# Rotary query copies in an attention kernel: spread over four heads, and in the first block over two queues

## Chip, cores and metric

The kernel runs on one core of a Trainium2 chip. The metric is the device time of one execution in microseconds; lower is better. Of several executions the median counts. A profiled execution also leaves a trace of every engine: TensorE (PE, matrix products; PEld are its weight loads), VectorE (DVE), ScalarE (ACT), GpSimd (POOL) and SyncE (SP), whose only work here is to issue DMA transfers.

## The reference

One layer of latent attention with 16 heads over 2048 positions of width 512, a layer norm after the residual, a linear layer with its residual and a second layer norm. What matters for the change is the attention: a query and a key have 128 parts without position and 64 parts with rotary position, and the key's rotary part is shared by all heads.

```python
cq = rms_norm(hidden_states @ w_qa.T, q_a_ln_w)
q = (cq @ w_qb.T).reshape(b, s, H, DQ).transpose(0, 2, 1, 3)
q_nope, q_pe = (q[..., :DN], q[..., DN:])
q_pe = q_pe * cos + rotate_half(q_pe) * sin
...
q_full = jnp.concatenate([q_nope, q_pe], axis=-1)
k_full = jnp.concatenate([k_nope, jnp.broadcast_to(k_pe, (b, H, s, DR))], axis=-1)
scores = jnp.einsum('bhqd,bhkd->bhqk', q_full, k_full) * scale
scores = jnp.where(causal, -jnp.inf, scores)
attn = jax.nn.softmax(scores.astype(jnp.float32), axis=-1).astype(q_full.dtype)
out = jnp.einsum('bhqk,bhkd->bhqd', attn, v)
```

## The kernel before

**Blocks, pairs, head steps.** The 2048 queries are four blocks of 512 (b = 0 to 3). A block goes through eight pairs of heads (p), a pair through four query tiles of 128 rows (qt), each with two heads (j). One head of one query tile is called a head step here; a pair has eight. In block 0 a pair's two heads are taken together, so there a step covers both. Because of the causal mask a step of block b covers up to 512(b+1) keys, so steps grow longer.

**Precision.** Numbers are carried as a high and a low part. A split makes the high part on ScalarE (line 64, a copy to a narrower format) and the low part on VectorE (line 65, the remainder). A product takes high by high, high by low and low by high.

**A head step.** TensorE computes scores (line 438): three products with the plain parts (`Kn,qn`) and two with the rotary parts (`Kp,pe`), where the rotary query stack `pe` of one head holds the high part on partitions 0 to 63 and the low part on 64 to 127. VectorE takes the negative maximum (line 510), ScalarE the exponential (line 532, tile `pr`). The probabilities are split into half-precision high (ScalarE, line 563) and low parts (GpSimd, line 564; lines 598 and 599 in block 0), transposed in squares by VectorE (line 546) back into `pr`, and copied by four DMA transfers (line 553) from `pr` into a ring buffer; in block 3 a step has two such tiles, so eight transfers. TensorE multiplies them with the values (line 619), ScalarE or VectorE copies the result out (lines 625, 628, tile `ot`), and a DMA transfer writes it to `ot_d` in memory.

**The rotary query part.** `project_pe(b, g)` makes it for four heads, that is two pairs: 18 matmuls (line 372, weights `wpe`), products with cosine and sine on VectorE (line 377, tile `prod`), a difference and a sum (lines 383, 384), a split into `ph` and the low part, which overwrites half of `prod`, and eight copies by DMA of 128 KB each into the stack tile `pe`: for every head j of the four its high part, then its low part. `project_nope(b, p)` does the plain part (line 410, weights `wq`). Both are generators, advanced in pieces between head steps, one pair ahead of their use (`project_pe` for the block's next two pairs, or in the block's last pair for the next block).

**Queues.** `state["queue"]` is GpSimd's queue through block 0, and SyncE's afterwards. Weight loads (`wq`, `wpe`, 768 KB each) go by it, and so do the output copies `ot_d`, by `put_off`. In block 0 the ring copies and the eight rotary copies (line 393) are issued by SyncE at the place where they stand. From block 1 on, `put_off(to, src, n)` puts a copy on a list, and `put_in` (line 326), called after the ring copies of each head step, issues by SyncE what has waited n calls and counts the others down; the start of each pair issues whatever is left. The rotary copies have n = 1, so all eight leave together, behind the ring copies of the second step after they were made.

**Numbers of copies.** Five groups are made while the queue is GpSimd's (four for block 0, one for block 1's first pairs), 40 copies; eleven groups follow, 88 copies.

**Order of the work.** In block 0 a scheduler lays out the order of all engines from a model of times. In blocks 1 to 3 the order of TensorE and SyncE, and from early in block 3 that of VectorE and ScalarE, is that of the program text. Every engine works through its instructions in order and waits at the first whose inputs or buffers aren't ready; this holds for the instructions that issue transfers too.

Of the kernel before, what the change touches and what calls it, by code (L numbers as in the profile page):

```python
# [49 lines left out]
def mla_block(ctx: ExitStack, tc: tile.TileContext, a, out):  # L50
    nc = tc.nc
# [9 lines left out]
    def split(ps, h, l, scale=None):  # L61

        if scale is None:
            nc.scalar.activation(h, ps, AF.Copy)  # L64
            nc.vector.tensor_tensor(l, ps, h.bitcast(F32), ALU.subtract)  # L65
        else:
            nc.scalar.activation(h, ps, AF.Copy, scale=scale)  # L67
            nc.vector.scalar_tensor_tensor(l, ps, scale, h.bitcast(F32), ALU.mult, ALU.subtract)  # L68
# [250 lines left out]
    def put_off(dst, src, n=0):  # L319

        if state["queue"] is nc.gpsimd:
            nc.gpsimd.dma_start(dst, src)
        else:
            later.append([n, dst, src])
# [29 lines left out]
    def load_wpe(b, g):  # L354
        if b == NB:
            return
        w = state["wpe", b, g] = prj.tile([P, 2, LT, 256], F32R, tag="wpe", name=f"wpe{b}_{g}")
        move(state["queue"], w, wpe_d[g])

    def project_pe(b, g, direct=None):  # L360

        if direct is None and ("wpe", b, g) not in state:
            load_wpe(b, g)
        w = state.pop(("wpe", b, g)) if direct is None else direct
        cq, cs = state["cq"], state["cs"]
        prod = prj.tile([P, 2, 2, QB], F32, tag="prod", name=f"prod{b}_{g}")
        for x in range(2):
            ps = psum["m"].tile([P, QB], F32, tag="m", name=f"ps_pe{b}_{g}_{x}")
            n = 0
            for lt in range(LT):  # L370
                for i, k in ((0, 0), (0, 1), (1, 0)):
                    nc.tensor.matmul(  # L372
                        ps, w[:, i, lt, x * P : (x + 1) * P], cq[:, k, lt, :], start=n == 0, stop=n == 8
                    )
                    n += 1
            for k in range(2):
                nc.vector.tensor_tensor(prod[:, k, x, :], ps, cs[:, k ^ x, :], ALU.mult)
            if x == 0:
                yield
            elif b or g == 3:  # L380
                load_wpe(*((b, g + 1) if g < 3 else (b + 1, 0)))
        rp, tp = prod[:, 0], prod[:, 1]
        nc.vector.tensor_tensor(rp[:, 0, :], rp[:, 0, :], rp[:, 1, :], ALU.subtract)
        nc.vector.tensor_tensor(rp[:, 1, :], tp[:, 0, :], tp[:, 1, :], ALU.add)
        ph, pl = prj.tile([P, 2, QB], F32R, tag="ph", name=f"ph{b}_{g}"), tp.bitcast(F32R)
        split(rp, ph, pl)
        pe = blk.tile([P, 4, QB], F32R, tag="pe", name=f"pe{b}_{g}")

        for j in range(4):
            for i, part in enumerate((ph, pl)):  # L390
                to, src = pe[64 * i : 64 * i + 64, j, :].bitcast(F32), part[32 * j : 32 * j + 32].bitcast(F32)
                if state["queue"] is nc.gpsimd:
                    nc.sync.dma_start(to, src)
                else:
                    put_off(to, src, 1)
        state["pe", b, g] = pe
        yield

# [24 lines left out]
    def project(b, p):  # L423
        if p % 2 == 0:
            yield from project_pe(b, p // 2)
        yield from project_nope(b, p)
# [249 lines left out]
    for _ in project_pe(0, 0, wpe0):  # L676
        pass
# [20 lines left out]
    def units(pool, ring, b):  # L698
        lag = min(ring.shape[1] // (2048 * (b + 1)) - 1, 3) if b else 2

        for p in range(NPAIR):
# [9 lines left out]
            if b and p % 2 == 0 and p + 2 < NPAIR:  # L711
                fillers.append(project_pe(b, p // 2 + 1))
# [431 lines left out]
```

## Time and profile before

| | |
|---|---|
| median of three executions | 1636.91 us (1634.71 to 1638.35) |
| profiled execution | 1638.56 us |
| its span in the trace | 1636.8 us |
| TensorE busy | 1575.2 us (96%) |
| VectorE, ScalarE, GpSimd busy | 1130.0, 918.3, 846.0 us (69%, 56%, 52%) |
| TensorE's waits for rotary copies (line 438) | 5.5 us, in one piece |
| TensorE's waits for ring copies (line 619) | 5.3 us, in one piece |
| issue of one rotary copy by SyncE in block 0, high or low | median 0.600 us |
| issue of one 128 KB output copy by GpSimd in block 0 | median 0.562 us |
| rotary copies in 245 to 262 us, issue to landing | high 4.3, low 7.9 us (medians of four) |

A row of the page for a group of instructions gives the line, the engine, the operation, output and inputs, shape, count, then busy time in us, the mean duration of one in ns, and the idle time of the engine before these instructions with what ended most of it. In a timeline a row gives start and duration in us, and in brackets the idle time before it and its releaser. PEclk is the share of full clock that TensorE was granted. The slices of the span (40 equal ones, some 41 us each, busy tenths) show where TensorE falls below nine tenths:

```profile
PE   9799998899999999999999999999999998999998
PEclk9899999999999999999999999999999999999999
DMA  6988676676776878787787767867777777962030
```

Block 0 lasts to about 250 us, block 3 begins at about 880 us, and its last result is written out at 1402 us; what is left of the output projection, the norms and the linear layer end the span.

### The profile page before, as it was taken

How to read it: one execution, taken by the hardware profiler on the slowest of the kernel's cores; microseconds unless marked ns; L12 is line 12 of the kernel's file. 1: busy time of each engine (PE TensorE's matmuls, PEld its weight loads, DVE VectorE, ACT ScalarE, POOL GpSimd, SP SyncE). 2: the span in 40 equal slices, each digit the busy share in tenths (PEclk: the TensorE clock that was granted, in tenths of full speed). 3: DMA queues.
4: the chain of work that ended last, by engine and by line, in shares of the span. 5: the costliest groups of instructions: out<-in, count | busy, mean ns of one | idle time of the engine just before them, and what ended most of it. 6: DMA issues, size and time to landing. Idle time of an engine off the chain costs nothing. (4 is left out here: it accounts for less than half of the span.)

```text
span 1636.8 us, 27536 instructions
## 1 busy us (share of the span) xinstructions
PE 1575.2 (96%) x9292; PEld 1294.5 (79%) x9292; DVE 1130.0 (69%) x1874; ACT 918.3 (56%) x1529; POOL 846.0 (52%) x701
## 2 busy tenths in 40 slices
PE   9799998899999999999999999999999998999998
PEld 7688876788888888888887778888887776678876
DVE  5668665577677777777777678778677676575464
ACT  5557564666665757666665665666666654321120
POOL 2345553454554766667765566666666665011011
PEclk9899999999999999999999999999999999999999
DMA  6988676676776878787787767867777777962030
GB/s 213 265 238 267 194 203 164 175 185 172 191 206 171 217 179 202 162 206 181 199 195 180 177 153 174 184 160 160 177 156 192 211 178 210 320 197 77 32 117 33
DMA packets 259436, 297.60 MB, mean 182 GB/s; under 512 B 35264, under 2 KB 227136, under 8 KB 258272
## 3 DMA queue, kind: packets, MB, share of 16 engines
q1 hardware_dynamic: 241008, 251.63, 55.4%
q0 software_dynamic: 11376, 34.52, 12.0%
q10 hardware_dynamic: 6912, 9.70, 2.0%
q8 instruction: 74, 1.21, 0.3%
q14 instruction: 66, 0.54, 0.1%
HBM read 99.94 MB, written 36.44 MB: 83 GB/s over the span
## 5 line engine op out<-in xcount | busy, mean ns | idle before, releaser
L564 POOL TENSOR_TENSOR hlpr<-pr,hlpr 128x1024 f16<-128x1024 f32 (+3 forms) x320 | 613.2, 1935 | 327.2 <-ACT hlpr L563 297.9
L438 PE MATMUL s<-Kn,qn 128*128 128x512 f32 (+4 forms) x1920 | 510.3, 373 | 22.3 <-ACT pr L532 13.9
L532 ACT ACTIVATE pr<-s,bias,rq 128x1024 f32<-128x1024 f32 (+3 forms) x320 | 325.4, 1021 | 343.2 <-issue 178.3
L510 DVE TENSOR_REDUCE neg<-s 128x1 f32<-128x1024 f32 (+3 forms) x320 | 310.0, 985 | 133.2 <-PE s L441 75.0
L438 PEld LDWEIGHTS s<-Kn,qn 128*128 128x128 f32 x1920 | 334.3, 189 | 72.7 <-ACT pr L532 19.9
L619 PE MATMUL o<-ring,V 128*128 128x256 f16 x3024 | 373.1, 273 | 7.4 <-DMA ring<-pr 5.3
L546 DVE STREAM_TRANSPOSE pr<-hlpr 128x1024 f32<-128x1024 f32 (+7 forms) x256 | 311.5, 1223 | 97.9 <-POOL hlpr L564 72.2
L438 PE MATMUL s<-Kp,pe 128*128 128x512 f32 (+4 forms) x1280 | 362.9, 364 | 5.5 <-DMA pe<-prod 5.5
L619 PEld LDWEIGHTS <-V 128*128 128x128 f16 x3264 | 301.1, 96 | 82.7 <-issue 32.0
L563 ACT ACTIVATE hlpr<-pr 128x1024 f16<-128x1024 f32 (+3 forms) x320 | 338.2, 1113 | 4.9 <-DVE pr L546 1.0
L438 PEld LDWEIGHTS s<-Kp,pe 128*128 128x128 f32 x1280 | 233.6, 189 | 36.4 <-DMA pe<-prod 5.7
L410 PE MATMUL ps_qn<-cq,wq 128*128 128x512 f32 x576 | 150.0, 405 | 2.1 <-DMA wq<-wq_d 1.9
L989 POOL TENSOR_TENSOR lnr<-lnt,nhalf 128x1 f32<-128x1 f32 x32 | 21.3, 671 | 213.3 <-DVE lnt L988 213.2
L410 PEld LDWEIGHTS ps_qn<-cq,wq 128*128 128x128 f32 x576 | 105.5, 192 | 23.1 <-DVE xl L65 1.1
L68 DVE SCALAR_TENSOR_TENSOR qn<-ps_qn,kvln,qn 128x512 fp32r<-128x512 f32 x64 | 47.5, 744 | 45.5 <-ACT qn L67 45.2
L599 POOL TENSOR_TENSOR hl<-pr,hl 128x128 f16<-128x128 f32 (+3 forms) x64 | 56.8, 908 | 37.7 <-ACT hl L598 37.3
L372 PE MATMUL ps_pe<-cq,wpe 128*128 128x512 f32 x288 | 75.3, 407 | 0.2 <-DMA cq<-cq_d 0.2
L64 ACT ACTIVATE oh<-o 128x1024 fp32r<-128x1024 f32 x28 | 29.7, 1061 | 79.6 <-PE acc L888 49.1
L888 PE MATMUL acc<-wvo,oh 128*128 128x512 f32 x224 | 71.5, 401 | 1.0 <-ACT pr L532 0.6
L64 ACT ACTIVATE xt<-tp 128x512 fp32r<-128x512 f32 x16 | 9.6, 598 | 94.8 <-PE tp L1008 94.8
L532 ACT ACTIVATION_READ_ACCUMULATOR pr<-s,bias,rq 128x1 f32 x320 | 61.8, 193 | 0.0
L372 PEld LDWEIGHTS ps_pe<-cq,wpe 128*128 128x128 f32 x288 | 53.4, 193 | 10.6 <-issue 0.3
(458 smaller groups left out, 1777.4 us busy)
## 6 DMA issues: line engine op xcount, KB each, us to landing
ring<-pr SPq DMA_DIRECT2D x384, 128.0 KB, 2.9
wq<-wq_d SPq DMA_DIRECT2D x22, 768.0 KB, 6.7
ring<-pr SPq DMA_DIRECT2D x128, 112.0 KB, 3.4
o<-ot_d SPq DMA_DIRECT2D x28, 512.0 KB, 5.5
ot_d<-ot SPq DMA_DIRECT2D x97, 128.0 KB, 2.7
ring<-pr SPq DMA_DIRECT2D x128, 96.0 KB, 2.4
ring<-pr SPq DMA_DIRECT2D x64, 192.0 KB, 4.1
ring<-pr SPq DMA_DIRECT2D x64, 176.0 KB, 5.3
```

Source lines behind the costliest of these rows:

```text
L68: nc.vector.scalar_tensor_tensor(l, ps, scale, h.bitcast(F32), ALU.mult, ALU.subtract)
L372: nc.tensor.matmul(ps, w[:, i, lt, x * P : (x + 1) * P], cq[:, k, lt, :], start=n == 0, stop=n == 8)
L410: nc.tensor.matmul(ps, w[:, i, lt, j * P : (j + 1) * P], cq[:, k, lt, :], start=n == 0, stop=n == 8)
L438: nc.tensor.matmul(ps[:, :w], lhs, K[:, i, c0 : c0 + w], start=n == 0, stop=n == 4 and not by_product)
L510: nc.vector.tensor_reduce(neg[:, ti : ti + 1], v, axis=AX.XY, op=ALU.max, negate=True)
L532: nc.scalar.activation(pr[:, x : x + n * w].rearrange("p (a c) -> p a c", a=n), v, AF.Exp, bias=bias, scale=r, accum_out=sums_of(b, p, qt, ...
L546: nc.vector.transpose(sq.rearrange("p (k c r) -> p k c r", k=4, r=32), words.rearrange("p (c k r) -> p k c r", k=4, r=32))
L563: nc.scalar.activation(hl[:, 0, c], pr[:, c], AF.Copy)
L564: nc.gpsimd.tensor_tensor(hl[:, 1, c], pr[:, c], hl[:, 0, c], ALU.subtract)
L599: nc.gpsimd.tensor_tensor(hl[:, j, 1, :], pr[:, j, :], hl[:, j, 0, :], ALU.subtract)
L619: nc.tensor.matmul(ps[:, :256], vt[:, i, k % 4, :], v[:, :, l, k, :], start=n == 0, stop=n == 3 * kts - 1)
L888: nc.tensor.matmul(acc, l[:, t, c], state["wvo"][p][:, i, j, :], start=p == 0 and j == 0 and n == 0, stop=p == NPAIR - 1 and j == 1 and n ...
```

## The change

In the branch for block 0 (and block 1's first group) the high copy of each head stays with SyncE and the low copy is issued by GpSimd: 20 of the 40 copies change queue. In the branch for blocks 1 to 3 the number of calls that a copy waits is 1 + j in place of 1, so the two copies of head 0 leave behind the step where all eight left, those of heads 1, 2 and 3 behind the next three steps, two at a time. Nothing else is edited; the order of block 0 is laid out anew by the scheduler.

```diff
             for i, part in enumerate((ph, pl)):
                 to, src = pe[64 * i : 64 * i + 64, j, :].bitcast(F32), part[32 * j : 32 * j + 32].bitcast(F32)
                 if state["queue"] is nc.gpsimd:
-                    nc.sync.dma_start(to, src)
+                    (nc.sync, nc.gpsimd)[i].dma_start(to, src)
                 else:
-                    put_off(to, src, 1)
+                    put_off(to, src, 1 + j)
```

In the order of instructions that results, the four low copies of the first group stand on GpSimd right behind the load of the second `wpe` tile, and those of block 1's first group behind a load of `wq` and half of a split of probabilities (line 599).

## The prediction

> **What bounds the kernel now.** I read the page's busy times first, then the costliest groups, then TensorE's waits, and last the timelines of SyncE's queue and of TensorE around the places where those waits stand.
>
> ```profile
> PE 1575.2 (96%) x9292; PEld 1294.5 (79%) x9292; DVE 1130.0 (69%) x1874; ACT 918.3 (56%) x1529; POOL 846.0 (52%) x701
> L438 PE MATMUL s<-Kp,pe 128*128 128x512 f32 (+4 forms) x1280 | 362.9, 364 | 5.5 <-DMA pe<-prod 5.5
> L619 PE MATMUL o<-ring,V 128*128 128x256 f16 x3024 | 373.1, 273 | 7.4 <-DMA ring<-pr 5.3
> ```
>
> TensorE is busy for 1575.2 of 1636.8 us, so nothing that leaves its work alone can win more than 61.6 us. The other two rows name the only long waits that the copies of rotary parts can be behind: one of 5.5 us for a low copy (`pe<-prod`), one of 5.3 us for the ring copies of probabilities, which share SyncE's queue with them. Over long stretches nothing can be won:
>
> ```profile
> 320.00:600.00 280.00, 279.11 (x1719) 230.18 (x1717) 201.41 (x314) 186.85 (x290) 158.80 (x95) 1.00 0.73 188
> 600.00:880.00 280.00, 280.00 (x1724) 230.85 (x1723) 214.21 (x377) 182.52 (x309) 191.02 (x148) 1.00 0.79 193
> 960.00:1240.00 280.00, 280.00 (x1707) 230.24 (x1705) 209.41 (x317) 178.38 (x234) 182.83 (x111) 1.00 0.74 169
> ```
>
> These are the windows by stretch (bounds, length, busy time of PE, PEld, DVE, ACT, POOL, granted clock, DMA share, GB/s). TensorE idles 0.9 us in 840, at full clock, although nine of the eleven bursts of copies of blocks 1 to 3 are issued there. Three places are left: the first score of block 1 (near 252 us), the first burst of block 1 (280 us) and the first of block 3 (913 us), besides block 0 itself.
>
> **Part 1: blocks 1 to 3, two copies behind each head step.** The number of copies stays 88 and each costs SyncE what it did; the starts below are 0.645 us apart, so a pair of them takes 1.29 us. Three pairs (3.87 us) leave the burst and go behind the next three head steps. What stood behind the burst goes earlier: the ring copies of the first step by 3.87 us, of the second by 2.58, of the third by 1.29, of the fourth by nothing. SyncE's timeline of the first burst, and TensorE's beside it:
>
> ```profile
> 280.52 0.61 SPq L330 DMA_DIRECT2D pe<-ph  x1
> 281.17 0.60 SPq L330 DMA_DIRECT2D pe<-prod  x1
> ...
> 285.68 0.58 SPq L330 DMA_DIRECT2D ot_d<-ot  x1
> 286.51 0.56 SPq L59 DMA_DIRECT2D wq<-wq_d  x1
> 287.17 12.72 SPq L553 DMA_DIRECT2D ring<-pr  x16
> ```
>
> ```profile
> 287.28 0.69 PE L438 MATMUL s<-Kn,qn 128*128 128x320 f32 x3
> ...
> 294.33 2.08 PE L619 MATMUL o<-ring,V 128*128 128x256 f16 x9 [5.27 <-DMA ring<-pr]
> 296.06 1.15 PE L438 MATMUL s<-Kn,qn 128*128 128x320 f32 x3
> 297.01 0.73 PE L438 MATMUL s<-Kp,pe 128*128 128x320 f32 x2
> ...
> 298.39 1.16 PE L619 MATMUL o<-ring,V 128*128 128x256 f16 x9
> ```
>
> The probabilities wait for SyncE: their copies start only when eight copies, an output copy and a weight load are through, and TensorE stands 5.27 us. After the wait the rows are slow: 2.08 against 1.16 us, 1.15 against 0.69, 0.73 against 0.46 in an undisturbed row of the same shape, 1.65 us in all; the granted clock is 0.83 over 290 to 300. So the place costs 6.9 us. If every later tile had slack, all of it would go: 3.87 us of the wait at once and with a shorter idle its slow rows too. If none had, TensorE would meet the third step's copies, which come only 1.29 us earlier. The second step's gain, 2.58, lies between and is the next thing TensorE meets (the o matmuls at 298.39 stood without a wait, but close behind). I take -2.6, ends -1.3 and -6.9.
>
> At the start of block 3 the same burst delays ScalarE, whose probabilities want a buffer that the ring copies still read:
>
> ```profile
> 926.11 1.10 ACT L532 ACTIVATE pr<-s,bias,rq 128x896 f32<-128x896 f32 x1 [3.14 <-DMA ring<-pr]
> ...
> 934.43 1.21 ACT L532 ACTIVATE pr<-s,bias,rq 128x1024 f32<-128x1024 f32 x1 [2.38 <-DMA ring<-pr]
> ```
>
> ```profile
> 932.11 0.96 PE L438 MATMUL s<-Kn,qn 128*128 128x512 f32 x3 [0.66 <-ACT pr L532]
> ...
> 948.14 0.72 PE L438 MATMUL s<-Kn,qn 128*128 128x320 f32 x3 [2.31 <-ACT pr L532]
> ...
> 949.98 3.95 PE L619 MATMUL o<-ring,V 128*128 128x256 f16 x21
> ```
>
> Both ScalarE waits are shorter than the 3.87 and about equal to the 2.58 by which those copies move. TensorE loses 0.66 and 2.31 us to late probabilities and 1.45 us to the slow row (3.95 against 2.50 us of the same 21 matmuls at 934.61): 4.4 us. The 2.31 comes 12 us after the last ring wait and may be due to the order around it, not to the copies. I take half of the 4.4, rounded down to -2.0, ends 0 and -4.4.
>
> What is moved behind other work must not be late itself: heads 2 and 3 of a group score a whole pair (eight steps) later than heads 0 and 1, and the last two copies go three steps after the first. Across a block boundary they go one step, about 7 us, before the next group's products overwrite their sources, against a median landing of 2.7 us. I cost this at nothing; its cover is that step, and without it the products at line 377 would wait some 3 us, once at each of two boundaries.
>
> **Part 2: block 0, low copies by GpSimd.** Twenty copies leave SyncE (20 x 0.60 = 12.0 us, by the median row at line 393) and come onto GpSimd. GpSimd's nearest issue is the output copy of the same 128 KB, 0.54 to 0.64, median 0.562 us: 20 x 0.562 = 11.2 us, in 250 us in which it is about half busy, so mostly beside other work. GpSimd is in order: its key additions, its splits of probabilities (line 599) and its output copies stand behind the wait for the low part, which VectorE makes (line 65). The scheduler lays block 0 out anew for all engines. TensorE idles some 15 us there from 60 to 240 us, in pieces under 3 us; I cost the shuffle at 0, ends -3 and +3 (a fifth of that idle).
>
> At the first group the four low copies now stand right behind a weight load of 768 KB in GpSimd's queue, issued at 49.8 and landed 8.8 us later, 58.6. TensorE's first use of the stack is at 58.17, so up to +1; against it ScalarE loses a wait of 1.8 us for such a copy (line 259), which ended in a TensorE wait of 2.75 at 63.05. I take 0, ends -1.8 and +1.
>
> At the boundary the group for block 1 meets the weight load `wq`:
>
> ```profile
> 249.15 0.85 POOL L59 DMA_DIRECT2D wq<-wq_d  x1
> 257.77 0.90 PE L438 MATMUL s<-Kp,pe 128*128 128x320 f32 x2 [5.48 <-DMA pe<-prod]
> wq<-wq_d POOLq DMA_DIRECT2D x1, 768.0 KB, 9.9
> pe<-ph SPq DMA_DIRECT2D x4, 128.0 KB, 4.3
> pe<-prod SPq DMA_DIRECT2D x4, 128.0 KB, 7.9
> ```
>
> The low part is ready at 249.9 (line 65 on VectorE, 248.74 plus 1.18). Issued by SyncE, head 0's copy is used at 257.77; the high ones took 4.3 us, the low ones 7.9 beside the load. The instruction order of the changed kernel puts these four behind that load in the load's own queue. If a queue is served from the front, head 0's copy lands just after the load, 249.15 + 9.9 = 259.05, plus at most 2 us for the copies: +1.3 to +3.2. If the load is quicker, because half the copies that shared the engines with it now stand behind it, or if copies overtake it, the landing is at best that of the high ones, 249.9 + 4.3 = 254.2: -3.5. The load's own row is the nearest, shortened a little: +0.5.
>
> One rule speaks against this part. The Trainium skill, "SBUF — State Buffer", section "A bandwidth-pool intuition that's wrong (but worth ruling out)", says that a transfer issued by GpSimd can be held until VectorE frees a shared port, with about 620 ns alone becoming some 3100. In this trace GpSimd's 31 output copies issue in 0.642 us at most while VectorE is more than half busy, so I see no such hold in the issue. By the page's figure my estimate is 2.5 us more for each copy; with one on the path at each of two places the sum below would be +0.9 in place of -4.1.
>
> **Sum.** 0.5 (boundary) + 0 (first group) + 0 (shuffle) - 2.6 (block 1) - 2.0 (block 3) = -4.1 us. The profiled execution took 1638.56 us (span 1636.8, so 1.8 around it), 1.65 above the median of 1636.91. Against its own time the forecast is 1634.5; carried to the median, **1632.8**. The terms' ends do not all fall together; the forecast's own range is -9 to 0, 1628 to 1637.
>
> **Rivals.** (a) *The stall moves on.* SyncE issues as many copies as before, so the backlog is only put off: block 1 wins its lower end, 1.3, block 3 nothing, and the boundary loses 1.3. For it: 16 ring copies stood in one unbroken row of 12.72 us. Against it: TensorE runs 840 us behind the same bursts without waiting. 0.0, so 1636.9.
>
> (b) *GpSimd's queue is late: slower.* The low copies land behind the 768 KB loads at the first group and at the boundary. The slowest landing from SyncE's put-off copies was 12.4 us; with that, after an issue at 50.5, the first use waits until 62.9 (+4.7), and after one at 251.5, held by the load and a split before it, until 263.9 (+6.1). 10.8 - 4.6 = +6.2: 1643.1. It decides once the two are late by 4.6 + 3.3 = 7.9 us together. For it: the order of that queue. Against it: the load itself took 8.8 and 9.9 us.
>
> (c) *All three places go.* The boundary ends at its best (-3.5, and half of the slow rows behind it, -1.5), blocks 1 and 3 at theirs (-6.9, -4.4): -16.3, 1620.6. For it: SyncE is freed of 12 us in block 0. Against: the copies' order behind the load.
>
> (d) *Nothing on the path changes*, as in the nine bursts that cost nothing; that is (a) in time.
>
> **How the numbers follow.** A difference of 0.2% (3.3 us) is about what a measurement of this kernel can tell from none. Forecast 0.40, (a) with (d) 0.23, (b) 0.25, (c) 0.12. Faster: 0.7 of the forecast and all of (c), with a little of (a), 0.44; slower: (b) and a little of (a) and the forecast's edge, 0.28; the rest, 0.28, is within 0.2%. The range runs from near (c), 1623, to just past (b), 1644; the forecast's own is above.
>
> **What would show it.** Right: the o matmuls near 294 wait less than 2.7 us for ring copies, ScalarE's waits of 3.14 and 2.38 near 926 and 934 shrink, and the first score of block 1 waits 4 to 8 us for a low copy by GpSimd. Wrong: waits for such copies inside block 0 (line 438), a new wait of products at line 377 at a block's start, a longer slow-clock stretch after the boundary, or GpSimd issues well over 0.6 us.

## The result, and the profile after

The changed kernel took 1650.91 us (median of five, 1644.09 to 1652.11) against 1637.54 us for the kernel before in the same comparison: a ratio of 1.007, 95% interval 1.0043 to 1.0097. It is slower by some 13 us where 4 us less were forecast, and lies above the forecast range. A second measurement gave the same ratio, 1.0069 (1.0043 to 1.0095).

The busy times and TensorE's longest waits in the changed kernel (line of the waiting instruction, what it waited for, us in total, times, longest):

```profile
PE 1584.0 (96%) x9292; PEld 1301.9 (79%) x9292; DVE 1136.9 (69%) x1874; ACT 918.5 (56%) x1529; POOL 855.3 (52%) x721
```

```profile
PE s L438 <- DMA pe<-prod: 7.4, 3, 5.9
...
PE ps_pe L372 <- DVE prod L377: 3.5, 1, 3.5
PE ps_qn L410 <- DMA wq<-wq_d: 3.3, 2, 3.1
PE o L619 <- DVE pad L471: 2.8, 1, 2.8
PE o L619 <- DVE prod L377: 2.8, 1, 2.8
```

TensorE has the same 9292 matmuls and is busy 8.8 us longer, at a mean granted clock of 0.985 against 0.990; the clock is lowest behind new waits (0.66 over 165 to 175 us, where the kernel before has 1.00, and 0.83 over 530 to 540). The ring wait of 5.3 us is gone from the top. New are waits behind the products of line 377 and a longest wait of 3.1 us for a weight load (0.9 before). The wait for the first low copy of block 1 is about what it was, 5.9 us.

Where the time goes is read best from how much later TensorE reaches its nth matmul than in the kernel before. The table is worked out from the traces (us; column heads are the times of that matmul before; in block 0 the scheduler changes the order, so there it says how much work was done, not which):

```
                    155    249    268    320    500    560    870    920    970   1360
changed            +2.2   +9.8  +10.6  +10.4  +10.4  +15.5  +16.9  +19.2  +14.3  +14.7
changed, again     +3.2  +10.7  +11.9   +8.0   +7.7  +11.3  +11.3  +13.5   +8.4   +7.6
GpSimd alone       +5.3  +12.9  +12.0  +13.3  +12.7  +13.0  +13.0  +13.3   +8.9   +5.0
spreading alone    +1.1   +3.0   +3.1   -1.2   -0.9   +4.5   +4.5   +5.5   +0.2   -0.9
spread in block    +1.6   +3.9   +3.3   -0.1   -0.2   -0.2   -0.2   -1.6   -6.9   -7.4
GpSimd, in block   +3.9  +11.0   +9.8   +9.0   +9.2   +9.2   +9.2   +7.3   +2.9   +4.8
loads by SyncE     +0.9   +3.1   +1.5   +2.9   +3.2   +3.3   +3.3   +1.3   -1.8   -3.2
one group          +3.6   +4.7   +6.0   +5.6   +5.4   +6.1   +6.1   +5.1   +0.3   +1.6
low first          +2.7   +2.6   +1.7   +3.8   +3.5   +3.3   +3.2   +1.3   -2.2   -4.3
load behind        -0.1   +1.2   -6.1   -4.4   -4.4   -4.4   -4.4   -6.0   -6.4   -5.4
```

Rows below the first belong to the experiments. Read the first: 10 us are lost before block 1, nothing in the first burst, 5 us at the start of block 2, 1.4 us soon after (in this profile alone), 2 us at the start of block 3; 5 us come back right after. Block 0 itself scatters: the rows that keep the order and queues of before (spreading alone, spread in block, low first) stand at +2.6 to +3.9 at 249 us, so the profile of before was at its lower end there, and the price of GpSimd's copies is nearer 8 than 10 us. A single profile is good to some 5 us there: two kernels of the experiments below with the same instructions in block 0 (low copies by ScalarE, without and with spreading) stand at +5.1 and +10.2 at 249 us, and at -4.6 and +0.5 at 268.

### The profile page after: what moved, and what is told of

It is laid out like the page before. It is cut to its first block, busy times and chain, and to the rows that moved or that the text cites. A ratio compares the mean times of both kernels' runs of the same rounds, so it can differ in the third digit from the quotient of the medians.

```text
span 1650.3 us, 27547 instructions
## 1 busy us (share of the span) xinstructions
PE 1584.0 (96%) x9292; PEld 1301.9 (79%) x9292; DVE 1136.9 (69%) x1874; ACT 918.5 (56%) x1529; POOL 855.3 (52%) x721
## 5 line engine op out<-in xcount | busy, mean ns | idle before, releaser
L410 PE MATMUL ps_qn<-cq,wq 128*128 128x512 f32 x576 | 153.4, 413 | 4.1 <-DMA wq<-wq_d 3.3
L67 ACT ACTIVATE qn<-ps_qn,kvln 128x512 fp32r<-128x512 f32 x64 | 43.7, 682 | 35.6 <-PE ps_qn L410 35.3
```

What stands on the lines that cost most here:

```text
L410: nc.tensor.matmul(ps, w[:, i, lt, j * P : (j + 1) * P], cq[:, k, lt, :], start=n == 0, stop=n == 8)
```

## Experiments

**1. One part alone.** The two edits of the change, each by itself:

```diff
 spreading alone:
-                    put_off(to, src, 1)
+                    put_off(to, src, 1 + j)
 GpSimd's part alone:
-                    nc.sync.dma_start(to, src)
+                    (nc.sync, nc.gpsimd)[i].dma_start(to, src)
```

> Only the spreading over four head steps; block 0's copies all by SyncE as before. Theory 1 (block 0's part costs the time): block 0 ends as before, first low-part score of block 1 again near 257.8 us; the spreading gains 4 us and gives it back near 300 to 310 us, loses 3.5 plus 1.6 us at the products (line 377) early in block 2, gains some 3 us in block 3: +1 to +4 us over before in all. Rival (the spreading costs it): +10 us or more.

> Only the low copies of block 0 by GpSimd; blocks 1 to 3 as before. Theory 1: the first low-part score of block 1 comes at some 269 us in place of 257.8, and the whole is +9 to +12 us; the wait for a weight load of 3.1 us near 165 us is there again, no wait for products at line 377 in block 2. Rival (the spreading costs it): within 3 us of before.

Spreading alone: 1635.51 us against 1638.37, ratio 0.9981 (0.9965 to 0.9997). GpSimd's part alone: 1641.41, ratio 1.002 (1.0008 to 1.0031). Spreading alone is thus some 3 us faster, where it was expected to be 1 to 4 us slower: the table shows 4.3 us won in the first burst of block 1 and not given back, and 5.4 us lost at the start of block 2, as expected. GpSimd's part alone costs 3 us, not the 9 to 12 that theory 1 has; by the total alone the rival would fit as well. The places speak for theory 1. GpSimd's part alone reaches the first low-part score of block 1 at 270.48 us (257.77 before), waits 3.28 us for the weights (line 410), and has no wait for products. It wins back 4.4 us at the start of block 3 and 3.9 us after 970 us, so 12 us of lateness become 3 us of time.

**2. The last pair of copies.** The spreading lets the two copies of head 3 go just before a block's end, where the next group's products are about to overwrite their source. The edit keeps that group's eight together (with g = 0 the first group of a block); once with block 0's copies by SyncE, once with GpSimd's part:

```diff
-                    put_off(to, src, 1 + j)
+                    put_off(to, src, 1 + j if g else 1)
```

> Spreading, but the first group of the next block goes all eight at once as before; block 0's copies by SyncE. If the 3.5 us wait for products at line 377 comes from the last pair of copies, which go just before the block's end, it is gone here and the kernel is 4 to 6 us faster than with the spreading alone: 1 to 4 us faster than before. If the wait has another source (the buffer of the products, the matmuls), it stays, and the two are the same.

> Both parts, but the next block's first group goes all eight at once as before. If the wait for products at line 377 early in block 2 costs the changed kernel what it cost the spreading alone, this is 4 to 6 us faster than the changed kernel; block 0 is as late as with GpSimd's part alone (first low-part score of block 1 near 269 us). If the wait is harmless there, the two are the same.

1631.46 us, ratio 0.9954 (0.994 to 0.9968), and with GpSimd's part 1638.06, ratio 0.9999 (0.9983 to 1.0016), where the changed kernel is at 1.0069. That is 4 us less than the spreading alone, as expected, and 10 us less than the changed kernel, where 4 to 6 were expected. VectorE's semaphore waits at line 377 (count, least, median and longest in ns) tell it most plainly; the changed kernel first, then the one spread in the block:

```profile
L377 DVEq EVENT_SEMAPHORE  x18: 21/50/4549, 37.4 to 896.6; - x18
```

```profile
L377 DVEq EVENT_SEMAPHORE  x10: 21/50/50, 36.8 to 877.5; - x10
```

The longest wait is 4.5 us where head 3's copies are late (5.0 us in the second profile of the changed kernel, 5.5 in the spreading alone), and 0.05 where they aren't. What it does at the start of block 2 in the changed kernel: SyncE's queue, then VectorE, then TensorE:

```profile
527.66 0.61 SPq L330 DMA_DIRECT2D pe<-ph  x1
528.31 0.82 SPq L330 DMA_DIRECT2D pe<-prod  x1
```

```profile
531.21 1.29 DVE L377 TENSOR_TENSOR prod<-ps_pe,cs 128x512 f32<-128x512 f32 x2 [3.98 <-issue]
```

```profile
532.55 3.91 PE L372 MATMUL ps_pe<-cq,wpe 128*128 128x512 f32 x9 [3.49 <-DVE prod L377]
```

The first nine matmuls of the group were done at 525 us. Their products wait until 531.21, 2.1 us after the issue of head 3's low copy ended; VectorE stands, since it works in order. (The profile names no releaser for its 3.98 us; that it is the copies is shown by the edit.) TensorE, whose next nine matmuls wait for these products, stops for 3.49 us and then runs at slow clock, 3.91 us for matmuls that take 2.31. The slow clock doesn't always follow: in the second profile of the changed kernel the same wait is 3.58 us long and the row behind it takes 2.37. The table shows +5.1 (500 to 560 us), +3.6 and +5.4 in the three profiles with late copies, and between -0.2 and +0.7 in the other rows. At the start of block 3 the same profiles lose 2.3, 2.2 and 1.0 us (870 to 920) where the rows spread in the block win 1.4 and 1.9. There VectorE stands about 1 us before these products, and TensorE waits 2.2 to 2.8 us behind line 377; but the kernel spread in the block has such a wait of 2.50 us too, so how much of this loss is the copies' isn't shown.

**3. Why block 0 is late.** Four kernels keep the burst of before and vary GpSimd's part: GpSimd's part as it is, but the weights of the plain parts (line 59, `wq`) by SyncE; the low copies by ScalarE's queue; by GpSimd only for block 1's first group; and all copies by SyncE, but each low copy ahead of its high one. Of the last three the replaced line isn't shown.

```diff
 loads by SyncE:
-        move(state["queue"], w, wq_d[p // 2][:, :, :, c0 : c0 + 256])
+        move(nc.sync, w, wq_d[p // 2][:, :, :, c0 : c0 + 256])
 by ScalarE, in place of GpSimd:
+                    (nc.sync, nc.scalar)[i].dma_start(to, src)
 one group:
+                    (nc.sync, nc.gpsimd if i and b else nc.sync)[i].dma_start(to, src)
 low first:
-            for i, part in enumerate((ph, pl)):
+            for i, part in (enumerate((ph, pl)) if state["queue"] is not nc.gpsimd else ((1, pl), (0, ph))):
```

> GpSimd's part alone, but the plain-part weights of block 0 (768 KB each) are loaded by SyncE in place of GpSimd. If block 0 loses its time because these loads stand behind the low copies and the other work of GpSimd, the 3 us wait for a weight load near 165 us is gone (under 1 us) and the low copies of block 1's first group, alone in GpSimd's queue, land sooner: 5 us or more less at the first score of block 1 than with GpSimd's part alone. If the lateness is the new order of all engines, block 0 ends as late as there.

> Only block 0's low copies moved, but to ScalarE's queue in place of GpSimd's; blocks 1 to 3 as before. If GpSimd is what makes block 0 late (its order and its queue of weight loads), the first score of block 1 comes within 4 us of before (about 254 to 262 us) and no wait of 3 us or more for a weight load stands near 165 us that before did not have. If any new order of block 0 costs as much, or the move off SyncE itself, it is 8 us late or more, as with GpSimd.

> Only the four low copies of block 1's first group by GpSimd, the sixteen of block 0's own groups by SyncE. If block 0 loses its time with its own groups, this one reaches its first wait for block 1's low copy at 252 to 256 us as before and waits 5 to 8 us there: 0 to +4 us in all. If the boundary is what costs, it is 8 us late or more after that wait.

> Block 0's copies all by SyncE, with the low one of each head before the high one: no work is added, moved to another queue or taken away, but the scheduler lays block 0 out anew. It shows what a new order alone can do: within 3 us of before at the first score of block 1 if such shuffles are small, as the prediction took them to be; 8 us or more if they are not.

| | median, us | ratio to before (95%) | first low-part score of block 1, us |
|---|---|---|---|
| loads by SyncE | 1636.32 | 1.0000 (0.9981 to 1.0018) | 260.26 |
| low copies by ScalarE | 1632.44 | 0.9964 (0.9947 to 0.998) | 255.85 |
| one group by GpSimd | 1638.50 | 0.9995 (0.998 to 1.001) | 263.75 |
| low first | 1638.86 | 1.0000 (0.9982 to 1.0018) | 259.49 |

In the four profiles (three kernels) in which GpSimd issues all twenty low copies and the loads that score came at 268.34 to 270.48 us; in those with block 0 as before at 257.77 to 261.89. Among these kernels block 0 is thus late when GpSimd has both the copies of its own groups and the weight loads; without the loads it isn't, and with one group only it is 2 to 6 us late at most, by a longer wait at the boundary (7.31 us). How one stands behind the other is seen on GpSimd near 155 us, in the changed kernel and then before:

```profile
155.52 2.15 POOL L393 DMA_DIRECT2D pe<-prod  x4
157.74 0.24 POOL L312 TENSOR_SCALAR rq<-rq 128x2 f32<-128x2 f32 x1
158.06 2.54 POOL L599 TENSOR_TENSOR hl<-pr,hl 128x512 f16<-128x512 f32 x2
160.55 0.60 POOL L322 DMA_DIRECT2D ot_d<-ot  x1
161.14 0.88 POOL L59 DMA_DIRECT2D wq<-wq_d  x1
```

```profile
154.36 2.55 POOL L599 TENSOR_TENSOR hl<-pr,hl 128x512 f16<-128x512 f32 x2 [1.58 <-ACT hl L598]
156.84 0.56 POOL L322 DMA_DIRECT2D ot_d<-ot  x1
157.40 0.86 POOL L59 DMA_DIRECT2D wq<-wq_d  x1
```

The load of weights leaves 3.7 us later, of which 2.15 are the four issues. TensorE, that comes for them 2.2 us later than before, waits 3.08 us instead of 0.94 (the changed kernel, then before):

```profile
168.38 4.18 PE L410 MATMUL ps_qn<-cq,wq 128*128 128x512 f32 x9 [3.08 <-DMA wq<-wq_d]
172.36 2.14 PE L619 MATMUL o<-PT,V 128*128 128x256 f16 x9
```

```profile
164.08 2.32 PE L410 MATMUL ps_qn<-cq,wq 128*128 128x512 f32 x9 [0.94 <-DMA wq<-wq_d]
```

Again slow rows follow: 4.18 and 2.14 us for work of 2.32 and 1.19. The wait alone doesn't tell the kernels apart, though: for these weights the kernels spread in the block and "load behind" (experiment 4), with their copies by SyncE, waited 2.62 and 2.41 us. From 155 to 200 us the four late profiles lose 3.1 to 4.8 us, and those with TensorE's order of before 0.4 to 3.4. What sets the four apart more clearly stands after that load: from 200 to 249 us they lose another 2.8 to 4.1 us, where the kernels with TensorE's order of before stay between -1.1 and +0.9. TensorE waits there some 2.1 us for probabilities near 225 us and 1.2 to 1.5 near 242 (line 584), and not for weights; before has one such wait, of 1.2 us. In the changed kernel:

```profile
224.75 0.62 PE L438 MATMUL s<-Kn,qn 128*128 128x384 f32 x2 [2.07 <-ACT pr L584]
```

What is shown is that in these kernels the loss comes only with both on GpSimd, the loads and the low copies; how its 8 us divide between this load, the splits of probabilities behind the copies (line 599) and the new order of all engines is not settled. "Low first" left TensorE's order as it was, so it doesn't test the last of these, and moving the loads to SyncE gave block 0 yet another order. The low copies by ScalarE do test it: its block 0 is laid out quite differently, 5.1 us late at 249 us, and makes that up, since other work of block 0 then stands where the others wait for the landing (no wait at the first low-part score at all). So a new order need not cost; whether this one does is open.

**4. The wait at the boundary.** The kernel before, with the weights of block 1's second pair issued by SyncE behind the eight copies:

```diff
-        move(state["queue"], w, wq_d[p // 2][:, :, :, c0 : c0 + 256])
+        move(nc.sync if (b, p) == (1, 1) else state["queue"], w, wq_d[p // 2][:, :, :, c0 : c0 + 256])
```

> The kernel before with one load changed: the 768 KB weights for block 1's second pair go by SyncE right behind the eight rotary copies, not by GpSimd beside them. If the 5.5 us wait at the first score of block 1 is due to that load sharing the transfer engines, the low copies land in some 4 us as the high ones did and the wait falls by 3 us or more (254 to 255 us for that score), with up to 1.5 us less of slow clock: -3 to -5 us in all. If the wait is set by how late VectorE makes the low part, or by the ring buffers' copies, it stays above 4 us.

1630.86 us, ratio 0.9953 (0.9937 to 0.9969): some 7 us, where 3 to 5 were expected. The transfers of 245 to 262 us and the first low-part score (KB each and median us to landing):

```profile
wq<-wq_d SPq DMA_DIRECT2D x1, 768.0 KB, 6.1
...
pe<-ph SPq DMA_DIRECT2D x4, 128.0 KB, 3.4
pe<-prod SPq DMA_DIRECT2D x4, 128.0 KB, 2.9
```

```profile
254.29 0.56 PE L438 MATMUL s<-Kp,pe 128*128 128x320 f32 x2 [0.55 <-DMA pe<-prod]
```

The low copies landed in 2.9 us in place of 7.9, the wait fell from 5.48 to 0.55 us, and the slow rows after it are gone (0.56 in place of 0.90). It was the load beside them that made them late.

**5. The gains together.** Spread in the block with the load behind the copies; and spread in the block with the low copies by ScalarE; and the changed kernel once more:

> Spreading within a block, next block's first group at once, block 0's copies by SyncE, and the weights of block 1's second pair by SyncE behind them. The two gains sit at different places (block 1's first score; the first bursts of blocks 1 and 3), so they should add: 11 to 14 us faster than before. If they are the same slack counted twice, 6 to 8 us.

> The change with both of its faults mended: block 0's low copies by ScalarE's queue, spreading within a block, the next block's first group all at once. If the gains of the two (some 6 and 7 us alone) sit at different places they add: 11 to 14 us faster than before, like the version that moves the weight load. If both win the same ring wait near 287 to 300 us, 7 to 9 us.

> The changed kernel once more, beside the runs of the kernel before on the same chip. If the two parts add (about -3 for the spreading alone, +3 for GpSimd's part alone), it is within 3 us of before, and the first measurement was a poor sample; if they hurt each other, it is again 10 to 14 us slower.

The first took 1625.03 us against 1636.81, ratio 0.9926 (0.9908 to 0.9944): the two gains, some 7 us each alone, add for the most part to 12, and it beats both kernels, the changed one by some 23 us. The second took 1631.37 against 1636.33, ratio 0.996 (0.9942 to 0.9977): 5 us, less than either expectation and than each of its gains alone; why is open. The changed kernel repeated at 1.0069 although its parts alone are at 0.9981 and 1.002, so these don't add either. By the ratios GpSimd's part costs some 3 us with the burst of before, 7 with the copies spread in the block and 15 with them spread as in the change; so taking either fault away undoes the whole loss. The table shows one reason: each part alone wins 4.4 or 5.3 us between 920 and 970 us, and both together win 4.9, once. The rest, 3.9 us that GpSimd's part alone wins after 970 us, has no explanation here; it comes after 1240 us, where TensorE of the kernel before idles 4.0 us in 60.

## Why the prediction was wrong

Added up from the table, the changed kernel lost 9.8 us by 249 us and 0.8 at the boundary, won 0.2 in the first burst, lost 6.5 from 500 to 870 us and 2.3 at the start of block 3, won 4.9 behind it and lost 0.4 after: 14.7 us where the sum of the prediction has -4.1. Nearly all of the miss lies in two terms that were taken at nothing.

**What bounds the kernel, and the boundary: right. The first group and block 1: within the scatter.** The boundary was taken at +0.5; the wait went from 5.48 to 5.89 (6.14 and 6.37 in the spreading alone and spread in the block, whose block 0 is as before). The first group was taken at 0; the changed kernel is 0.3 us later by 80 us, the other three profiles with these copies and the loads on GpSimd 2.2 to 3.1, but "low first" 1.8 without them. For the first burst of block 1 the forecast was -2.6 with ends -1.3 and -6.9: from 268 to 320 us the kernels with spread copies in the table won 0.2 (the changed one), 3.9 (again), 4.3, 3.4 and 0.8 us; those with the burst changed by -0.4 to +2.1. So the gain is there in most of them, but in the changed kernel's first profile it is below the lower end of 1.3. There the stall seems to have moved on, as rival (a) feared: the wait of 5.27 us is gone, and these two stand behind its place.

```profile
302.50 1.16 PE L619 MATMUL o<-ring,V 128*128 128x256 f16 x9 [2.80 <-DVE pad L471]
...
310.06 1.30 PE L619 MATMUL o<-ring,V 128*128 128x256 f16 x9 [2.04 <-DMA ring<-pr]
```

**The shuffle of block 0, "0, ends -3 and +3": the first step that failed.** The term that failed is the cost of laying twenty issues onto GpSimd, which was put at nothing. The issues themselves were sized well: 0.535 to 0.610 us each, by the median row 0.568 where 0.562 was taken. They were called "mostly beside other work", and the list of what stands behind them named key additions, splits and output copies, but not the weight loads. Those are on GpSimd too, TensorE needs each at a fixed place, and they are large. Measured: some 8 us more than kernels with the old order lose in block 0, in four profiles that agree within 3 us. Rival (b) had the queue of GpSimd as the slow side, but the other way round: copies late behind loads. In this trace a load left late behind the copies, and at the boundary the copies landed in 7.2 us, no slower than the 7.9 of before. That load explains part of the loss at most; where the rest comes from stays open (experiment 3).

**The products, "I cost this at nothing; its cover is that step": the second.** The price without cover was given (3 us at each of two boundaries), and the wait was named among the signs of being wrong. The runs show it: 3.49 us and slow rows, 5.1 us, at the first; at the second 2.3 us, of which the copies' share isn't known. The cover wasn't there. The step was taken as some 7 us between issue and next writing, against a landing of 2.7 us. But head 3's low copy stands in SyncE's queue behind the other steps' ring copies, and its issue ended at 529.1 us, when the matmuls whose products need the room had been done for nearly 4 us.

**Block 3, -2.0: a gain came, its cause is open.** From 920 to 970 us the changed kernel won 4.9 us, but so did kernels with the whole burst there (GpSimd alone 4.4, one group 4.8, low first 3.5), and one didn't (load behind, 0.4). So most of what was lost there isn't the burst's. Near that place VectorE's order, laid out by the scheduler, differs between these kernels and the one before; but "low first" and "load behind" have the same order of VectorE and of ScalarE from block 1 on, and one won 3.5 us and the other 0.4, so that order alone isn't the cause. That the term came out with the right sign is luck.

The Trainium skill's rule that VectorE can hold up transfers issued by GpSimd ("SBUF — State Buffer", section "A bandwidth-pool intuition that's wrong (but worth ruling out)") isn't what these runs show: no issue took longer than 0.610 us, and the loss goes when the loads are moved and the copies stay with GpSimd.

## What to carry to other kernels

When transfers are given to another engine, list everything behind them there that something else waits for, the large loads first, and not only whether the engine has idle time. When copies are spread out, look at who overwrites their source: the last one's landing, not its issue, is the date by which that buffer is free, and a block's end is where the room is least. A large load that isn't urgent belongs behind the small urgent copies, in their queue: that one edit was worth 7 us here, more than the 5 us that the prediction allowed the change there at best.

## What had not been expected of the hardware

Block 0 ends at different times in profiles of kernels that have the same instructions in it for TensorE (+1.2 to +3.9 us in five of them against the profile of before, and +5.1 and +10.2 in the two with the low copies by ScalarE), and single executions of one kernel lie 4 to 15 us apart (spreading alone 1629.07 to 1643.84). A profile of one execution can't settle a term of 2 us in such a stage.

Two waits of nearly the same length at the same place of the same kernel can differ in what follows: behind 3.49 us the granted clock was 0.80 over 528 to 536 us and the row took 3.91 us, behind 3.58 us it was 1.00 and the row took 2.37.
